# Scores ahead of other work on VectorE in the first two groups of a graph-attention kernel

## The chip, the cores and the metric

The kernel runs on one core of one Trainium2 chip. A core has five engines that run side by side, each with its own queue of instructions, and they wait for one another through semaphores. TensorE multiplies matrices into PSUM, an accumulator memory of eight banks. VectorE and ScalarE can read PSUM. [...] SyncE issues the transfers between the chip's large memory (HBM) and SBUF, the working memory. The metric is the device time of one execution in microseconds, as the median of several runs. In the profile the engines are called PE, DVE, ACT, POOL and SP, and PEld is TensorE's loading of weights, which overlaps its products.

## The reference: what is computed

There are 128 graphs of 128 nodes with 768 features each. One layer of masked attention with 12 heads of 64 features is added to the input:

```python
h = jnp.maximum(_layernorm(x, axis=-1), 0.0)
q = _split_heads(h @ Wq + bq)
k = _split_heads(h @ Wk + bk)
v = _split_heads(h @ Wv + bv)
scores = jnp.einsum('bhqd,bhkd->bhqk', q, k) / sqrt(64)
adj_e = adj[:, None, :, :]
scores = scores + beta * adj_e
scores = jnp.where(adj_e > 0, scores, -9e15)
probs = softmax(scores, axis=-1)
out = x + (einsum('bhqk,bhkd->bhqd', probs, v), heads merged)
```

Everything is in float32. About one in eight entries of adj is positive.

## The kernel before

The kernel works on groups of four graphs, 32 groups in all. A group passes through three slices: `qk0` (q and k of heads 0 to 5), `v`, and `qk1` (q and k of heads 6 to 11). In a slice the large product of activations and weights is made from 15 block products with fewer multiplications than the 18 of the plain scheme, at the cost of sums of activation blocks (`S...`) and of weight blocks (`T...`). The weight sums are made once, in the first group; the activation sums in every group. The first slice of group 0 is computed plainly with 18 products, because its sums are not there yet.

The sums of weights and of activations, all on VectorE, one instruction of 512 elements per partition each:

```python
SUMS_B = (
    ("T9", "-B01", "B12", -1), ("T2", "B01", "B02", 1), ("T2", "T2", "B22", 1), ("T10", "B10", "B12", 1),
    ("T0", "B00", "B02", 1), ("T12", "-B00", "B12", -1), ("T6", "T0", "B22", 1), ("T7", "T10", "B21", -1),
    ("T1", "T6", "B20", 1), ("T1", "T1", "B21", -1), ("T4", "T10", "B20", -1), ("T11", "B11", "B12", 1),
    ("T11", "T11", "B21", -1), ("T13", "B11", "B01", -1), ("T13", "T13", "T10", -1),
)
SC_AT = 1              # scores are issued behind product 1 of a slice
AV_AT = (5, 8, 11)     # attention blocks behind products 5, 8 and 11
HT_AT = {"A01": 0, "A00": 1, "A11": 2, "A02": 3, "A10": 4, "A12": 9}
```

(The three comments are added here; in the kernel these lines stand without them.)

A block product keeps adding into the bank of its chain (`a` to `d`). After each product the partial sum is read: the first reading of a target goes to ScalarE for q and k, every later one is an addition on VectorE. So a product waits until the reading of the earlier one of its chain is done:

```python
def product(G, sl, n, order):
    an, bn, chain, uses = PRODUCTS[n]
    ...
    nc.tensor.matmul(p[q:q + HD, i, :], lhs[:, q:q + HD], rhs, start=(first and i == 0 and c == 0), ...)     # L331
    ...
    for (r, j), sign in uses:
        ...
        elif key not in qk:
            ...
            nc.scalar.activation(t[:, i, :], p[:, i, :], AF.Identity, bias=bqk[:, i, oc:oc + 1], scale=float(sign))   # L352
        else:
            t = qk[key]
            added[G] = nc.vector.tensor_tensor(t, t, p, ALU.add if sign > 0 else ALU.subtract)    # L356
    if n == mine[-1]:
        give(banks.pop(chain))
```

The list of products gives the chain of each. For the steps that the text below speaks of: P2, P7, P11 and P14 share chain b, P0, P3, P6, P9 and P12 share chain c.

The scores of six heads take six of the eight banks at once. VectorE takes each bank out, caps the scores and adds the bias; ScalarE makes the exponential:

```python
def scores(G, u):
    order = (3 * u, 3 * u + 2, 3 * u + 1)
    ps = {(oc, i): take() for oc in order for i in range(2)}
    for oc in order:
        ...     # score matmuls, L377
        for i in range(2):
            e = es[G, oc, i] = work.tile(...)
            nc.vector.scalar_tensor_tensor(e, ps[oc, i]..., SCORE_CAP * ISCALE, biasT[G], op0=ALU.min, op1=ALU.add)   # L381
            give(ps[oc, i])
            nc.scalar.activation(e, e, AF.Exp, scale=1.0 / ISCALE)                                                    # L384
```

The bias is made from adj on VectorE, with its square on ScalarE; the maximum of the square only feeds a guard at the end (`seen_b`), which decides whether a general version has to run again:

```python
def bias_1(G, raw):
    ...
    nc.vector.transpose(a, raw...)                        # L298
    nc.vector.tensor_scalar(kp, a, 0.0, None, op0=ALU.is_gt)
    nc.vector.tensor_scalar(a, a, beta_c, ...)
    nc.gpsimd.memset(t, MASKED)
    nc.vector.copy_predicated(t, kp, a)
    nc.scalar.activation(a, a, AF.Square)                 # L305
    return a

def bias_2(G, a):
    nc.vector.tensor_reduce(bm, a, AX.X, ALU.max)         # L310
    nc.vector.tensor_tensor(seen_b, seen_b, bm, ALU.max)  # L311
```

The attention block multiplies the exponentials with V (which carries a column of ones, so that the sum comes along), and `weigh` divides:

```python
def weigh(G, oc, r, pa, o):
    nc.vector.tensor_scalar(sm, pa[:, :, HD:VE], TINY, None, op0=ALU.max)
    nc.vector.reciprocal(rs, sm)
    nc.vector.tensor_mul(o, pa[:, :, 0:HD], rs.to_broadcast([P, 4, HD]))      # L392
    for i, t in enumerate((sm, rs)):
        nc.vector.tensor_tensor(s, s, ..., ALU.max)

def attend(G, oc):
    for r in range(2):
        ...                               # matmuls, L406
        weigh(G, oc, r, pa, o[:, r])
        give(bank)
    nc.gpsimd.tensor_add(t, t, o...)      # L411
    nc.sync.dma_start(out[...], t)
```

The order of work is written as lists of what is to be issued behind which product (`then(n, f)`). The framework may move an instruction ahead on its engine when its inputs are early; `tc.issue_after(i)` holds it behind instruction `i`. In the first two groups:

```python
if G + 1 < NG:
    for g in range(GRP):
        then(6, lambda g=g: load_x(G + 1, g, (nc.sync,)))
        if G:
            then(11 + g, lambda g=g: stats(G + 1, g))                          # slice qk0
...
if G == 1:
    for n in range(8, len(SUMS_B)):
        then(n - 8, lambda n=n: sum_weights("qk0", n))                         # slice qk0
...
then(10, lambda: bias_2(0, behind_adds(bias_1, 0, adj_0)))                     # slice v of group 0
...
def transposes(n):
    with tc.issue_after(added[G].ins):
        to_hT(G + 1, int(n[1]), int(n[2]))                                     # slice qk1
if not G:
    for n in range(8):
        then(n, lambda n=n: behind_adds(sum_weights, "qk0", n))                # slice qk1
    then(13, lambda: bias_2(1, behind_adds(bias_1, 1, load_adj(1))))
```

Of the kernel before, what the change touches and what calls it, by code (L numbers as in the profile page):

```python
# [13 lines left out]
AF = mybir.ActivationFunctionType  # L14
ALU = mybir.AluOpType
AX = mybir.AxisListType

P = 128
HEADS = 12
GRP = 4  # L20
# [4 lines left out]
SCORE_CAP = 60.0  # L25
# [6 lines left out]
def kernel(  # L32
# [56 lines left out]
# [6 lines that stand above are left out]
# [6 lines left out]
SC_AT = 1  # L101
# [10 lines left out]
def direct(ctx, tc, x, adj, wq, bq, wk, bk, wv, bv, beta, out, bad):  # L112
# [10 lines left out]
    nc = tc.nc  # L123
    B, N, D = x.shape
    HD = D // HEADS
# [6 lines left out]
    ISCALE = math.sqrt(HD)  # L132
# [13 lines left out]
    xg, A, biasT, vt, qk = {}, {}, {}, {}, {}  # L146
# [51 lines left out]
    def sum_weights(sl, n):  # L198
        name, a, b, sign = SUMS_B[n]
        if (sl, name) not in wt:  # L200
            raw = [r for r, home in HOME.items() if home == name]
            wt[sl, name] = wt[sl, raw[0]] if raw else const.tile([P, 2, H2], F32, name=f"{sl}_{name}")
        if a[0] == "-":
            nc.vector.scalar_tensor_tensor(wt[sl, name], wt[sl, a[1:]], -1.0, wt[sl, b], op0=ALU.mult,
                                           op1=ALU.add if sign > 0 else ALU.subtract)
        else:
            nc.vector.tensor_tensor(wt[sl, name], wt[sl, a], wt[sl, b], ALU.add if sign > 0 else ALU.subtract)
# [80 lines left out]
    def load_adj(G):  # L288

        t = work.tile([P, GRP, NB, SQ], F32, tag="adj", name=f"adj_{G}", bufs=1)  # L290
        src = adj[G * GRP:(G + 1) * GRP].rearrange("g (b i) (a j) -> a i (g b) j", i=SQ, a=NB)
        for a in range(NB):
            nc.sync.dma_start(t[a * SQ:(a + 1) * SQ].rearrange("p g b j -> p (g b) j"), src[a])
        return t
# [13 lines left out]
    def bias_2(G, a):  # L308
        bm = stat.tile([P, GRP], F32, tag="bm", name=f"bm_{G}", bufs=1)
        nc.vector.tensor_reduce(bm, a, AX.X, ALU.max)  # L310
        nc.vector.tensor_tensor(seen_b, seen_b, bm, ALU.max)  # L311

    banks, added = {}, {}
# [43 lines left out]
        if n == mine[-1]:  # L357
            give(banks.pop(chain))

    es, xo = {}, {}  # L360

    def load_xo(G, oc):
        t = xo[G, oc] = work.tile([P, GRP, P], F32, tag="xo", name=f"xo_{G}_{oc}", bufs=3)
# [2 lines left out]
# [6 lines that stand above are left out]
                t = qk[G, f"qk{u}", g // 2, oc % 3]  # L372
                at = slice((g % 2) * N, (g % 2 + 1) * N)
                for i in range(2):
                    r = slice(i * HD, (i + 1) * HD)
                    for k in range(0, N, HD):
                        nc.tensor.matmul(ps[oc, i][k:k + HD, g * N:(g + 1) * N], t[r, 1, at][:, k:k + HD], t[r, 0, at],  # L377
                                         start=True, stop=True)
            for i in range(2):
                e = es[G, oc, i] = work.tile([P, GRP, N], F32, tag="e", name=f"e_{G}_{oc}_{i}", bufs=6)  # L380
                nc.vector.scalar_tensor_tensor(e, ps[oc, i].rearrange("p (g n) -> p g n", g=GRP), SCORE_CAP * ISCALE,  # L381
                                               biasT[G], op0=ALU.min, op1=ALU.add)
                give(ps[oc, i])
                nc.scalar.activation(e, e, AF.Exp, scale=1.0 / ISCALE)  # L384

    def weigh(G, oc, r, pa, o):

        sm = stat.tile([P, 4, 1], F32, tag="sm", name=f"sm_{G}_{oc}_{r}")
        nc.vector.tensor_scalar(sm, pa[:, :, HD:VE], TINY, None, op0=ALU.max)
        rs = stat.tile([P, 4, 1], F32, tag="rs", name=f"rs_{G}_{oc}_{r}")  # L390
        nc.vector.reciprocal(rs, sm)
        nc.vector.tensor_mul(o, pa[:, :, 0:HD], rs.to_broadcast([P, 4, HD]))  # L392
        for i, t in enumerate((sm, rs)):
            s = seen[:, i, 4 * r:4 * r + 4]
            nc.vector.tensor_tensor(s, s, t.rearrange("p b e -> p (b e)"), ALU.max)
# [95 lines left out]
    adj_0 = load_adj(0)  # L491
# [22 lines left out]
    def after(f, *args):  # L514

        with tc.issue_after(first["dve"].ins), tc.issue_after(first["pool"].ins):
            return f(*args)
# [11 lines left out]
    def behind_adds(f, *args):  # L529

        with tc.issue_after(added[0].ins):
            return f(*args)

    for G in range(NG):
        todo = attention(G - 1, 1) if G else {}

        def then(n, f):
            todo.setdefault(n, []).append(f)

        if G:  # L540
            todo.setdefault(SC_AT, []).insert(0, lambda: scores(G - 1, 1))

        if G + 1 < NG:
            for g in range(GRP):
                then(6, lambda g=g: load_x(G + 1, g, (nc.sync,)))
                if G:
                    then(11 + g, lambda g=g: stats(G + 1, g))
        if not G:
            load_weights("qk1")
            with tc.issue_after(first["dve"].ins):  # L550
                half(1, 0)
            then(1, lambda: half(1, 1))
            then(2, lambda: half(1, 2))
            for n in range(len(SUMS_A)):
                then(n + 5, lambda n=n: after(sum_acts, 0, n))
            for n in range(len(SUMS_B)):
                then(n // 2 + 5, lambda n=n: after(sum_weights, "v", n))
            plain_slice(0, "qk0", todo)
        else:
            if G == 1:  # L560
                for n in range(8, len(SUMS_B)):
                    then(n - 8, lambda n=n: sum_weights("qk0", n))
            slice_of(G, "qk0", todo)
        todo = {SC_AT: [lambda: scores(G, 0)]} if G else {}
        if G + 1 < NG:
            got = []
            at = 3 if G else 6
            for g in range(GRP):
                if not G:
                    then(g, lambda g=g: stats(G + 1, g))  # L570
                then(at + 5 + g, lambda g=g: norm(G + 1, g))
            then(at, lambda: got.extend(moments_1(G + 1, 0, GRP * NB)))
            then(at + (3 if G else 2), lambda: moments_2(G + 1, 0, GRP * NB, *got[:2]))
            if G:
                then(8, lambda: got.append(bias_1(G + 1, load_adj(G + 1))))
                then(12, lambda: bias_2(G + 1, got[2]))
            else:
                for n in range(len(SUMS_B)):
                    then(n, lambda n=n: behind_adds(sum_weights, "qk1", n))
                then(10, lambda: bias_2(0, behind_adds(bias_1, 0, adj_0)))  # L580
        slice_of(G, "v", todo)
        todo = attention(G, 0)
        if not G:
            todo.setdefault(SC_AT, []).insert(0, lambda: scores(0, 0))

        def transposes(n):
            with tc.issue_after(added[G].ins):
                to_hT(G + 1, int(n[1]), int(n[2]))

        if not G:  # L590
            for n in range(8):
                then(n, lambda n=n: behind_adds(sum_weights, "qk0", n))
            then(13, lambda: bias_2(1, behind_adds(bias_1, 1, load_adj(1))))
        if G + 1 < NG:
            for n, at in HT_AT.items():
                then(at, lambda n=n: transposes(n))
            for n, at in enumerate(SUMS_AT):
                then(at, lambda n=n: sum_acts(G + 1, n))
        if G + 1 < NG:
            slice_of(G, "qk1", todo)  # L600
            continue

        todo = {}
        for at, f, *args in (
            (0, load_xo, 0), (0, load_xo, 1), (0, load_xo, 2), (0, attend, 0), (2, attend, 2), (4, attend, 1),
            (9, scores_half, 5, 0), (10, scores_half, 4, 0), (11, attend_half, 5, 0), (12, scores_half, 3, 0),
            (12, attend_half, 4, 0), (13, scores_half, 3, 1), (13, attend_half, 3, 0), (14, scores_half, 5, 1),
            (14, attend_half, 3, 1), (14, scores_half, 4, 1), (14, attend_half, 5, 1), (14, attend_half, 4, 1),
        ):
            then(at, lambda f=f, args=args: f(G, *args))  # L610
        slice_of(G, "qk1", todo, LAST)
# [142 lines left out]
```

## Time and profile before

| | |
|---|---|
| median of 3 runs | 2917.83 us (2917.03 to 2917.94) |
| span of the profiled execution | 2913.8 us |
| TensorE's granted clock over the span | 0.998 of full speed |
| slice qk0 of group 0 (plain) | 15.96 to 48.08 us |
| slice v of group 0 | 48.08 to 74.57 us |
| slice qk1 of group 0, with scores 0 | from 74.57 us; score matmuls at 78.55 us |
| scores 1, in slice qk0 of group 1 | score matmuls at 114.94 us |
| VectorE busy, 78.5 to 84.4 us | 5.90 of 5.90 us |
| VectorE busy, 84.4 to 114.9 us | 30.50 of 30.50 us |
| VectorE busy, 158 to 190 us | 17.79 of 32.00 us |

A row of a timeline is a run of equal instructions: its start, its length, the engine, the line of the kernel, the operation, what is written and what is read, their shapes and the count. A bracket gives the idle time of the engine just before it and who ended it. A row of the table by windows gives for each engine the busy time and, in brackets, the number of instructions, in the order PE, PEld, DVE, ACT, POOL; then the granted clock of TensorE, the busy share of the DMA engines and the rate in GB/s.

### The profile page before, as it was taken

Reading aid. Unit: us, or ns where it says so; the run is one execution under the profiler, and the core shown is the slowest. Engines: PE = TensorE matmul, PEld = TensorE weight load, DVE = VectorE, ACT = ScalarE, POOL = GpSimd, SP = SyncE. Lnnn points to the kernel's source line nnn. Section 1 sums busy time; section 2 is a strip of 40 time slices with the busy share of each in tenths; the row PEclk is TensorE's granted clock in tenths of the full one; section 3 lists DMA queues with packets and bytes.
Section 4 is the critical chain, followed back from the end, with each engine's and each line's share of the span. In section 5 each row is a group of like instructions: output and inputs, shape, how many; then the busy total and the mean of one; then the engine's idle time right before and its main releaser. Section 6 shows DMA issues by size and latency. Waiting matters only on the chain.

```text
span 2913.8 us, 81848 instructions
## 1 busy us (share of the span) xinstructions
PE 2881.5 (99%) x35526; PEld 2017.0 (69%) x35526; DVE 1993.8 (68%) x5155; ACT 796.6 (27%) x1703; POOL 376.0 (13%) x307
## 2 busy tenths in 40 slices
PE   8899999999999999999999999999999999999998
PEld 6666676666676666766667666677667776666766
DVE  7866676766677666776667676677766677666765
ACT  2322222323223232222222232322323222222221
POOL 1111111111111111111111111111111111111110
PEclk9999999999999999999999999999999999999999
DMA  6211122111222212222112212122121222111211
GB/s 164 71 52 46 51 70 69 50 55 48 61 70 56 58 38 61 71 59 56 45 52 70 67 50 55 45 65 70 52 61 38 61 70 59 56 45 49 67 41 38
DMA packets 358622, 172.22 MB, mean 59 GB/s; under 512 B 84464, under 2 KB 358128, under 8 KB 358256
## 3 DMA queue, kind: packets, MB, share of 16 engines
q1 hardware_dynamic: 355392, 166.14, 21.0%
q8 instruction: 280, 4.59, 0.7%
q10 hardware_dynamic: 2864, 0.79, 0.1%
q14 instruction: 86, 0.70, 0.1%
HBM read 116.53 MB, written 50.33 MB: 57 GB/s over the span
## 4 chain that ended last, share of the span: by engine, by line
PE 81%; issue 8%; DVE 5%; DMA 2%; POOL 2%; SPq 1%; ACT 0%; ACTq 0%; POOLq 0%; DVEq 0%
PE bank L331 70%; PE bank L406 5%; PE bank L377 5%; DMA x<-in_x_dram 2%; DVE S L285 1%; PE bank L477 1%; POOL xo L411 1%; POOL rstd L261 1%; DVE qk L356 1%; DVE st L227 1%; DVE A L279 1%; DVE o L392 0%; SPq L152 0%; DVE e L381 0%; ACT x L272 0%
## 5 line engine op out<-in xcount | busy, mean ns | idle before, releaser
L331 PE MATMUL bank<-S,qk_T 128*64 128x256 f32 x7056 | 825.5, 380 | 13.3 <-DVE e L381 11.9
L331 PEld LDWEIGHTS bank<-S,qk_T 128*64 128x64 f32 x7056 | 503.9, 137 | 273.4 <-DVE e L381 16.4
L356 DVE TENSOR_TENSOR qk<-qk,bank 128x512 f32<-128x512 f32 x630 | 430.4, 683 | 347.0 <-PE bank L331 346.7
L352 ACT ACTIVATE qk<-bank,bqk 128x256 f32<-128x256 f32 x756 | 313.4, 471 | 1010.4 <-PE bank L331 870.1
L331 PE MATMUL bank<-S,qk_B 128*64 128x256 f32 x4032 | 478.1, 379 | 0.9 <-DVE qk L356 0.9
L331 PE MATMUL bank<-A,qk_T 128*64 128x256 f32 x4032 | 478.5, 379 | 0.3 <-DVE qk L356 0.3
L411 POOL TENSOR_TENSOR xo<-xo,o 128x512 f32<-128x512 f32 x189 | 256.1, 1355 | 1608.5 <-DVE o L392 1029.7
L331 PE MATMUL bank<-v_T,S 128*64 128x256 f32 x3584 | 422.7, 380 | 0.0
L384 ACT ACTIVATE e<-e 128x512 f32<-128x512 f32 x378 | 227.6, 630 | 684.4 <-DVE e L381 683.9
L347 DVE TENSOR_TENSOR v<-v,bank 128x512 f32<-128x512 f32 x320 | 220.1, 688 | 264.7 <-PE bank L331 264.6
L331 PEld LDWEIGHTS bank<-A,qk_T 128*64 128x64 f32 x4032 | 283.8, 137 | 137.3 <-DVE qk L356 0.4
L331 PEld LDWEIGHTS bank<-S,qk_B 128*64 128x64 f32 x4032 | 278.1, 137 | 129.3 <-DVE qk L356 1.4
L331 PEld LDWEIGHTS bank<-v_T,S 128*64 128x64 f32 x3584 | 252.2, 137 | 126.4 <-issue 5.7
L272 ACT ACTIVATE x<-x,shift,rstd 128x192 f32<-128x192 f32 x512 | 228.0, 533 | 343.6 <-POOL shift L263 343.6
L331 PE MATMUL bank<-v_B,S 128*64 128x256 f32 x2048 | 244.7, 380 | 0.0
L381 DVE SCALAR_TENSOR_TENSOR e<-bank,biasT 128x512 f32<-128x512 f32 x378 | 231.5, 681 | 13.5 <-PE bank L377 13.5
L331 PE MATMUL bank<-v_T,A 128*64 128x256 f32 x2048 | 238.3, 379 | 0.0
L342 DVE TENSOR_TENSOR v<-bv_b,bank 128x512 f32<-128x512 f32 x192 | 131.9, 687 | 145.8 <-PE bank L331 145.8
L406 PEld LDWEIGHTS bank<-v,e 128*64 128x64 f32 x6048 | 208.5, 138 | 27.4
L279 DVE STREAM_TRANSPOSE A<-x 128x256 f32<-128x256 f32 x384 | 215.6, 613 | 7.6 <-ACT x L272 7.4
L227 DVE BATCH_NORM_STATS2 st<-x 128x6 f32<-128x192 f32 x512 | 160.8, 349 | 76.1 <-DMA x<-in_x_dram 75.6
L406 PE MATMUL bank<-v,e 128*64 128x65 f32 x6048 | 208.3, 221 | 0.0
(79 smaller groups left out, 1724.7 us busy)
## 6 DMA issues: line engine op xcount, KB each, us to landing
x<-in_x_dram SPq DMA_DIRECT2D x504, 96.0 KB, 2.5
xo<-in_x_dram SPq DMA_DIRECT2D x189, 256.0 KB, 2.8
out_dram<-xo SPq DMA_DIRECT2D x189, 256.0 KB, 2.2
adj<-in_adj_dram SPq DMA_DIRECT2D x128, 64.0 KB, 2.4
qk_T<-in_L_gnn_Wq_dram SPq DMA_DIRECT2D x10, 128.0 KB, 3.4
qk_T<-in_L_gnn_Wk_dram SPq DMA_DIRECT2D x10, 128.0 KB, 3.4
v_T<-in_L_gnn_Wv_dram SPq DMA_DIRECT2D x5, 256.0 KB, 5.9
qk_B<-in_L_gnn_Wq_dram SPq DMA_DIRECT2D x8, 128.0 KB, 3.4
```

The source lines that it names most:

```text
L227: nc.vector.bn_stats(st[G][:, g * NB + b, :], xg[G, g][:, b, :])
L272: nc.scalar.activation(t, t, AF.Relu, bias=shift[G, n], scale=rstd[G, n])
L279: last = nc.vector.transpose(t[:, :, g * N:(g + 1) * N].rearrange("p c (b i) -> p c b i", i=SQ), src)
L331: nc.tensor.matmul(p[q:q + HD, i, :], lhs[:, q:q + HD], rhs, start=(first and i == 0 and c == 0), stop=(c == 1), skip_group_check=True)
L347: added[G] = nc.vector.tensor_tensor(o, o, got, ALU.add if sign > 0 else ALU.subtract)
L352: nc.scalar.activation(t[:, i, :], p[:, i, :], AF.Identity, bias=bqk[:, i, oc:oc + 1], scale=float(sign))
L356: added[G] = nc.vector.tensor_tensor(t, t, p, ALU.add if sign > 0 else ALU.subtract)
L377: nc.tensor.matmul(ps[oc, i][k:k + HD, g * N:(g + 1) * N], t[r, 1, at][:, k:k + HD], t[r, 0, at], start=True, stop=True)
L381: nc.vector.scalar_tensor_tensor(e, ps[oc, i].rearrange("p (g n) -> p g n", g=GRP), SCORE_CAP * ISCALE, biasT[G], op0=ALU.min, op1=ALU.add)
L384: nc.scalar.activation(e, e, AF.Exp, scale=1.0 / ISCALE)
L406: nc.tensor.matmul(pa[q:q + HD, 2 * g + i, :], es[G, oc, i][:, 2 * r + g, q:q + HD], vt[G, "v", r, h // 4][:, 4 * g + h % 4, :], start=Tru ...
L411: nc.gpsimd.tensor_add(t, t, o.rearrange("p a (b j) d -> p (a b) (j d)", j=2))
```

## The change

In the first two groups VectorE has additional work: sums of weights, and for group 1 its transposes and sums of activations in a hurry. The change orders this work so that VectorE takes the scores first. It has five parts:

- `taken[0]` remembers the last taking of scores; `behind_scores` holds work behind it. Weight sums of `qk0`, the transposes of group 1 and the statistics of group 2 go behind the scores of their slice.
- Nine weight sums in place of eight are made in slice qk1 of group 0, from product 2 on; the other six in slice qk0 of group 1, from product 2 on.
- The bias maximum of groups 0 and 1 is made a slice later than the bias itself, behind the scores.
- In group 0 the first V outputs are divided on ScalarE: four copies of 64 elements with a scale per half block, in place of one multiplication of 256 elements on VectorE.
- The rest stays as it was: the division from group 1 on, the transposes that group 1 and later groups make for the next one, the bias maximum from group 2 on.

What is computed stays the same.

```diff
@@ -357,7 +357,7 @@
         if n == mine[-1]:
             give(banks.pop(chain))
 
-    es, xo = {}, {}
+    es, xo, taken = {}, {}, {}
 
     def load_xo(G, oc):
         t = xo[G, oc] = work.tile([P, GRP, P], F32, tag="xo", name=f"xo_{G}_{oc}", bufs=3)
@@ -378,8 +378,8 @@
                                          start=True, stop=True)
             for i in range(2):
                 e = es[G, oc, i] = work.tile([P, GRP, N], F32, tag="e", name=f"e_{G}_{oc}_{i}", bufs=6)
-                nc.vector.scalar_tensor_tensor(e, ps[oc, i].rearrange("p (g n) -> p g n", g=GRP), SCORE_CAP * ISCALE,
-                                               biasT[G], op0=ALU.min, op1=ALU.add)
+                taken[0] = nc.vector.scalar_tensor_tensor(e, ps[oc, i].rearrange("p (g n) -> p g n", g=GRP), SCORE_CAP * ISCALE,
+                                                          biasT[G], op0=ALU.min, op1=ALU.add)
                 give(ps[oc, i])
                 nc.scalar.activation(e, e, AF.Exp, scale=1.0 / ISCALE)
 
@@ -389,7 +389,11 @@
         nc.vector.tensor_scalar(sm, pa[:, :, HD:VE], TINY, None, op0=ALU.max)
         rs = stat.tile([P, 4, 1], F32, tag="rs", name=f"rs_{G}_{oc}_{r}")
         nc.vector.reciprocal(rs, sm)
-        nc.vector.tensor_mul(o, pa[:, :, 0:HD], rs.to_broadcast([P, 4, HD]))
+        if G:
+            nc.vector.tensor_mul(o, pa[:, :, 0:HD], rs.to_broadcast([P, 4, HD]))
+        else:
+            for b in range(4):
+                nc.scalar.activation(o[:, b], pa[:, b, 0:HD], AF.Copy, scale=rs[:, b])
         for i, t in enumerate((sm, rs)):
             s = seen[:, i, 4 * r:4 * r + 4]
             nc.vector.tensor_tensor(s, s, t.rearrange("p b e -> p (b e)"), ALU.max)
@@ -531,6 +535,12 @@
         with tc.issue_after(added[0].ins):
             return f(*args)
 
+    def behind_scores(f, *args):
+
+        with tc.issue_after(taken[0].ins):
+            return f(*args)
+
+    early = []
     for G in range(NG):
         todo = attention(G - 1, 1) if G else {}
 
@@ -543,7 +553,9 @@
         if G + 1 < NG:
             for g in range(GRP):
                 then(6, lambda g=g: load_x(G + 1, g, (nc.sync,)))
-                if G:
+                if G == 1:
+                    then(11 + g, lambda g=g: behind_scores(stats, G + 1, g))
+                elif G:
                     then(11 + g, lambda g=g: stats(G + 1, g))
         if not G:
             load_weights("qk1")
@@ -558,8 +570,9 @@
             plain_slice(0, "qk0", todo)
         else:
             if G == 1:
-                for n in range(8, len(SUMS_B)):
-                    then(n - 8, lambda n=n: sum_weights("qk0", n))
+                for n in range(9, len(SUMS_B)):
+                    then(n - 7, lambda n=n: behind_scores(sum_weights, "qk0", n))
+                then(4, lambda: behind_scores(bias_2, 1, early[1]))
             slice_of(G, "qk0", todo)
         todo = {SC_AT: [lambda: scores(G, 0)]} if G else {}
         if G + 1 < NG:
@@ -577,23 +590,24 @@
             else:
                 for n in range(len(SUMS_B)):
                     then(n, lambda n=n: behind_adds(sum_weights, "qk1", n))
-                then(10, lambda: bias_2(0, behind_adds(bias_1, 0, adj_0)))
+                then(10, lambda: early.append(behind_adds(bias_1, 0, adj_0)))
         slice_of(G, "v", todo)
         todo = attention(G, 0)
         if not G:
             todo.setdefault(SC_AT, []).insert(0, lambda: scores(0, 0))
 
         def transposes(n):
-            with tc.issue_after(added[G].ins):
+            with tc.issue_after(added[G].ins if G else taken[0].ins):
                 to_hT(G + 1, int(n[1]), int(n[2]))
 
         if not G:
-            for n in range(8):
-                then(n, lambda n=n: behind_adds(sum_weights, "qk0", n))
-            then(13, lambda: bias_2(1, behind_adds(bias_1, 1, load_adj(1))))
+            for n in range(9):
+                then(n + 2, lambda n=n: behind_scores(sum_weights, "qk0", n))
+            then(5, lambda: behind_scores(bias_2, 0, early[0]))
+            then(13, lambda: early.append(behind_scores(bias_1, 1, load_adj(1))))
         if G + 1 < NG:
             for n, at in HT_AT.items():
-                then(at, lambda n=n: transposes(n))
+                then(at if G else max(at, SC_AT), lambda n=n: transposes(n))
             for n, at in enumerate(SUMS_AT):
                 then(at, lambda n=n: sum_acts(G + 1, n))
         if G + 1 < NG:
```

## The prediction

> **What bounds the kernel now.** I read the page's busy shares first, then TensorE's waits in the first 340 us, then the timelines of TensorE and VectorE over 78 to 128 us, then the granted clock there microsecond by microsecond. The shares:
>
> ```profile
> PE 2881.5 (99%) x35526; PEld 2017.0 (69%) x35526; DVE 1993.8 (68%) x5155; ACT 796.6 (27%) x1703; POOL 376.0 (13%) x307
> ```
>
> TensorE is busy for 2881.5 of 2913.8 us and its instruction order is the same in both programs. So only its gaps (32.3 us, of which about 16 us pass before its first product) and its slow stretches can be won. The waits of TensorE up to 340 us (us in total, times, longest):
>
> ```profile
> PE bank L238 <- DVE st L227: 7.7, 2, 5.8
> PE bank L331 <- DVE e L381: 6.9, 3, 3.6
> PE bank L331 <- DVE qk L356: 1.2, 2, 0.9
> ```
>
> The first belongs to the start-up, which the change leaves alone. The others are products (L331) that wait for a PSUM bank until VectorE has taken scores out of it (L381), or until it has added a finished partial sum to q and k (L356). Where they lie, in TensorE's timeline (start, length, in brackets the idle time before):
>
> ```profile
> 78.55 2.85 PE L377 MATMUL bank<-qk 64*64 64x128 f32 x96
> 84.48 3.67 PE L331 MATMUL bank<-S,qk_T 128*64 128x256 f32 x32 [3.08 <-DVE e L381]
> ...
> 105.04 1.95 PE L331 MATMUL bank<-A,qk_T 128*64 128x256 f32 x16 [0.27 <-DVE qk L356]
> 107.89 1.95 PE L331 MATMUL bank<-S,qk_B 128*64 128x256 f32 x16 [0.90 <-DVE qk L356]
> ...
> 121.39 6.46 PE L331 MATMUL bank<-S,qk_T 128*64 128x256 f32 x32 [3.59 <-DVE e L381]
> ```
>
> The score matmuls end at 81.40 us and TensorE stands until 84.48. After the second score block it stands for 3.59 us, and then 32 matmuls take 6.28 us (121.39 to the next row's start, 127.67) where 32 take 3.46 elsewhere. The granted clock (the column after POOL) says why:
>
> ```profile
> 119.00:120.00 1.00, 0.00 (x0) 0.00 (x0) 1.00 (x6) 0.11 (x1) 0.00 (x0) 1.00 0.15 19
> 120.00:121.00 1.00, 0.00 (x0) 0.00 (x0) 1.00 (x4) 0.00 (x0) 0.00 (x0) 0.62 0.06 8
> 121.00:122.00 1.00, 0.61 (x4) 0.43 (x6) 1.00 (x3) 0.57 (x1) 0.00 (x0) 0.50 0.00 0
> 126.00:127.00 1.00, 1.00 (x8) 0.48 (x6) 1.00 (x3) 0.34 (x1) 0.20 (x1) 0.50 0.00 0
> 127.00:128.00 1.00, 1.00 (x12) 0.70 (x10) 0.96 (x3) 0.05 (x1) 0.00 (x0) 0.97 0.14 24
> ```
>
> During the idle stretch the clock falls to half and stays there until about 127 us. VectorE's timeline shows what it did instead of taking the first scores:
>
> ```profile
> 78.03 0.69 DVE L310 TENSOR_REDUCE bm<-adjT 128x4 f32<-128x512 f32 x1 [3.48 <-ACT adjT L305]
> 79.31 0.68 DVE L347 TENSOR_TENSOR v<-v,bank 128x512 f32<-128x512 f32 x1
> 81.11 1.12 DVE L279 STREAM_TRANSPOSE A<-x 128x256 f32<-128x256 f32 x2
> 82.72 1.13 DVE L279 STREAM_TRANSPOSE A<-x 128x256 f32<-128x256 f32 x2
> 83.77 3.65 DVE L381 SCALAR_TENSOR_TENSOR e<-bank,biasT 128x512 f32<-128x512 f32 x6
> ```
>
> It stood 3.48 us in front of the bias maximum, whose square ScalarE delivers late, and only then worked off a sum of activations into V, weight sums and four transposes. From 78 to 126 us it has no idle gap.
>
> **What the Trainium skill says.** "TensorE: Matmul & The Clock Gate", section "What's actually happening", gives a free-running window of about 3.4 us: an idle window puts the clock at half, a busy one restores it. The trace agrees: 3.08 us idle kept full clock, 3.59 us lost it. "PSUM — Partial Sum Buffer", section "Engine vs sequencer instructions", says that the queues of ScalarE and VectorE are strict FIFO; the 3.48 us wait that held everything behind it is that. "ScalarE: Activation LUTs", section "What ACT_TABLE_LOAD costs", gives 186 ns + 0.833 ns per element, 93 ns more for each pointer operand, 93 ns of overlap back to back. Its 532 ns for the norms (192 elements, two pointers) fit the 533 ns in the trace. "SBUF — State Buffer", section "Who interferes with whom", says that a VectorE instruction with two SBUF inputs contends with a GpSimd one that reads SBUF. The trace has it: while GpSimd adds xo at 97.22, two sums of VectorE take 2.36 us in place of about 1.3.
>
> **The change part by part.** I number a slice's products P0 to P14; one takes 1.727 us (TensorE's row to row), an attention block 0.93.
>
> *Scores first, bias maximum out of the way.* With the maximum gone from this place, VectorE has finished its V sums and two weight sums by about 77.5 us. The first scores can be taken 1.14 us after the score matmuls begin (that lag is seen in group 1: matmuls at 153.02, taken at 154.16), so at 79.7. Six takings at 0.60 us end at 83.3. TensorE needs the first freed bank at 81.40 and has it at 80.4. The wait of 3.08 us goes: TensorE is ahead by 3.08.
>
> *Work put behind.* It must now be done between the two score blocks. Unhindered, TensorE would reach P14 at 81.40 + 12 x 1.727 + 3 x 0.93 = 104.9. P14 continues P11's bank, so it needs VectorE's addition of P11. In the new order there stand up to and with it: 6 takings, 7 additions, 9 weight sums and 9 activation sums, together 31 x 0.60 = 18.6; 12 transposes x 0.54 = 6.5; the bias maximum 0.6; four halves of attention statistics without their multiplication x 0.28 = 1.1. That is 26.8 us, from 79.7 to 106.5. GpSimd's additions of xo cross this span twice, at 1.1 us each if they meet two-input sums: 106.5 to 108.7, mean 107.6. P14 thus starts at 107.6 and not at 109.67. TensorE is 2.1 us ahead, and its waits for L356 grow from 1.2 to about 2.7.
>
> *The division on ScalarE.* The multiplication of 0.34 us leaves VectorE six times before the second scores (2.0 us; it is counted above by its absence) and six times after. ScalarE gets 48 copies of 64 elements with one pointer: by the skill's formula 186 + 93 + 53 - 93 = 239 ns each, an estimate, 11.5 us in all on an engine that is busy for 27%. The statistics of the first block come at 79.7 + 13.3 = 93.0, so eight copies end at 95.1; behind them in the queue is P6's copy to SBUF (0.84), which ends at 95.9. P9 would want that bank at 95.35: a wait of 0.5 us, which the wait at P14 swallows.
>
> *The second score block.* After P14 come two products of group 1, then scores: 107.6 + 3 x 1.727 + 0.1 = 112.9, ending at 115.75. VectorE has after P11's addition 0.6 of statistics, 2.0 of bias work, three additions and two sums (3.0): free at 113.2. The first scores are there at 112.9 + 1.14 = 114.0. It now meets neither 2.0 us of multiplications nor the statistics of group 2 (16 x 0.27 = 4.3 us, which the old order threads between the takings). So TensorE goes on at 115.75 without a wait, where it went on at 121.39: 5.6 us. No idle window, no half clock: another 6.28 - 3.46 = 2.8 us. Sum 8.4; without the contention 9.5. I take the middle, 9.0.
>
> *Afterwards.* Six weight sums and the statistics follow the takings (from 117.6). T4, needed at P8, is the second of them, and P8 starts at about 127. From 140 us on VectorE waits for TensorE in most rows, so the lead stays. The other waits for scores (5.2 us in nine places after 140 us) are in code that stays as it is.
>
> **The rivals.** *VectorE's backlog only moves the wait.* If its work between the score blocks takes 3 us more than counted, the second takings start late again, 1 to 3 us of idle return, and with over 3.4 us the half clock too. Then 3 to 5 us are left: 2913 to 2915. For it: VectorE has no gap there. Against it: 3.48 us of idling and 2.0 us of multiplications leave it, and 4.3 us of statistics move behind.
> *ScalarE becomes the step that is waited for.* If a copy costs 332 ns with no overlap, eight take 2.65 us, P9 waits 1.2 us, and later P6 of group 1 likewise: 1 to 2 us lost, 2910 to 2911. Against it: ScalarE's long gaps (18.12 us before 113.33).
> *A deferred weight sum or transpose comes late,* and TensorE waits for a product's operand: then 2910 or more. The margins are about 9 us for T4 and over 10 us for the first activation sums.
>
> **Range and chances.** 2917.83 - 9.0 = 2908.8. All waits in reach are 3.08 + 1.17 + 3.59 + 2.8 = 10.6 us, which puts the floor at 2907.2; with half a microsecond of scatter, 2906.7. The upper end takes half of the first rival: 2912.3. Two per cent are 58 us, more than all gaps of TensorE, and nothing here could cost as much: within 2% with 0.99.
>
> **What would show it.** Right: no wait of some 3 us at either score block; a granted clock of 1.00 from 78 to 130; the waits for L356 at 2 to 3 us; the first taking near 79.7 and the second block's near 114; ScalarE's copies at about 240 ns. Wrong: a wait named L381 over 1 us before 130 us, a clock below 1.00 there, or a new wait for L352, L207 or L285.

## The result and the profile after

| | before | after |
|---|---|---|
| median of 6 runs | 2916.97 us (2912.03 to 2917.94) | 2907.56 us (2905.17 to 2909.06) |
| ratio of the times, 95% interval | | 0.9970 (0.9957 to 0.9983) |
| span of the profiled execution | 2913.8 us | 2905.1 us |

The changed kernel is faster by 9.4 us, or 0.3%. That is clear of the scatter and far below 2%. The prediction was 2908.8 us.

TensorE's waits in the first 340 us of the changed kernel (us in total, times, longest). Because the change adds lines, L396 is now the division on ScalarE and L415 GpSimd's addition of xo:

```profile
PE bank L238 <- DVE st L227: 7.0, 2, 5.8
PE bank L481 <- DVE A L279: 2.2, 1, 2.2
PE bank L331 <- DVE qk L356: 1.8, 3, 0.9
PE bank L254 <- DVE dev L245: 0.5, 1, 0.5
PE bank L331 <- DVE e L381: 0.4, 1, 0.4
PE bank L331 <- ACT qk L352: 0.2, 1, 0.2
```

The waits for scores (L381) fell from 6.9 to 0.4 us. Those for additions to q and k (L356) grew from 1.2 to 1.8, and one for ScalarE is new. The timeline of TensorE shows where:

```profile
79.57 2.85 PE L377 MATMUL bank<-qk 64*64 64x128 f32 x96
82.35 3.67 PE L331 MATMUL bank<-S,qk_T 128*64 128x256 f32 x32
...
96.69 1.95 PE L331 MATMUL bank<-S,qk_B 128*64 128x256 f32 x16 [0.16 <-ACT qk L352]
...
103.38 1.95 PE L331 MATMUL bank<-A,qk_T 128*64 128x256 f32 x16 [0.36 <-DVE qk L356]
106.26 1.95 PE L331 MATMUL bank<-S,qk_B 128*64 128x256 f32 x16 [0.94 <-DVE qk L356]
108.67 3.67 PE L331 MATMUL bank<-S,qk_T 128*64 128x256 f32 x32 [0.46 <-DVE qk L356]
...
114.00 2.85 PE L377 MATMUL bank<-qk 64*64 64x128 f32 x96
116.78 3.67 PE L331 MATMUL bank<-S,qk_T 128*64 128x256 f32 x32
```

Both score blocks are followed by the next product at once: 82.35 is 2.78 us after 79.57, and 116.78 is 2.78 us after 114.00. In this execution everything stands 1.02 us later from the start on (first score matmul at 79.57 in place of 78.55; in the profiles of this study it lies between 78.34 and 80.29, whatever the kernel). The clock has a part in that too: the first 16 matmuls of the plain slice took 5.41 us here, with half clock from 15.86 to 19.27 us, and 3.72 us at full clock in the profile before. Times below are therefore counted from the first score matmul. VectorE, as far as the first score block:

```profile
76.83 0.68 DVE L207 TENSOR_TENSOR qk_T<-qk_T,qk_T 128x512 f32<-128x512 f32 x1
80.78 3.68 DVE L381 SCALAR_TENSOR_TENSOR e<-bank,biasT 128x512 f32<-128x512 f32 x6 [3.27 <-PE bank L377]
84.38 2.20 DVE L279 STREAM_TRANSPOSE A<-x 128x256 f32<-128x256 f32 x4
```

It is ready at 77.5 and stands for 3.27 us, now for the scores themselves. The granted clock (the column after POOL), where it had been half before:

```profile
120.00:121.00 1.00, 1.00 (x14) 0.64 (x10) 1.00 (x3) 0.50 (x2) 0.00 (x0) 1.00 0.00 0
121.00:122.00 1.00, 1.00 (x12) 0.65 (x10) 1.00 (x2) 0.34 (x1) 0.00 (x0) 1.00 0.00 0
126.00:127.00 1.00, 1.00 (x12) 0.69 (x10) 1.00 (x8) 0.58 (x3) 0.00 (x0) 1.00 0.00 0
```

### The profile page after: what moved, and what is told of

Same layout as the page of the kernel before. It is cut to its first block, busy times and chain, and to the rows that moved or that the text cites. A ratio compares the mean times of both kernels' runs of the same rounds, so it can differ in the third digit from the quotient of the medians.

```text
span 2905.1 us, 81884 instructions
## 1 busy us (share of the span) xinstructions
PE 2880.0 (99%) x35526; PEld 2016.3 (69%) x35526; DVE 1987.7 (68%) x5143; ACT 806.8 (28%) x1751; POOL 376.0 (13%) x307
## 4 chain that ended last, share of the span: by engine, by line
PE 81%; issue 9%; DVE 5%; DMA 2%; POOL 2%; SPq 1%; ACT 0%; POOLq 0%; DVEq 0%
PE bank L331 70%; PE bank L377 5%; PE bank L410 5%; DMA x<-in_x_dram 2%; PE bank L481 1%; POOL rstd L261 1%; POOL xo L415 1%; DVE S L285 1%; DVE qk L356 1%; DVE st L227 1%; DVE A L279 1%; DVE o L393 0%; SPq L152 0%; DVE e L381 0%; SPq L416 0%
## 5 line engine op out<-in xcount | busy, mean ns | idle before, releaser
L356 DVE TENSOR_TENSOR qk<-qk,bank 128x512 f32<-128x512 f32 x630 | 429.8, 682 | 344.9 <-PE bank L331 344.6
L352 ACT ACTIVATE qk<-bank,bqk 128x256 f32<-128x256 f32 x756 | 313.4, 471 | 992.8 <-PE bank L331 833.8
L415 POOL TENSOR_TENSOR xo<-xo,o 128x512 f32<-128x512 f32 x189 | 256.1, 1355 | 1606.9 <-DVE o L393 993.2
L381 DVE SCALAR_TENSOR_TENSOR e<-bank,biasT 128x512 f32<-128x512 f32 x378 | 231.2, 680 | 16.7 <-PE bank L377 16.7
L279 DVE STREAM_TRANSPOSE A<-x 128x256 f32<-128x256 f32 x384 | 215.5, 612 | 7.6 <-ACT x L272 7.4
```

The costliest lines, as they stand in the source:

```text
L279: last = nc.vector.transpose(t[:, :, g * N:(g + 1) * N].rearrange("p c (b i) -> p c b i", i=SQ), src)
L381: taken[0] = nc.vector.scalar_tensor_tensor(e, ps[oc, i].rearrange("p (g n) -> p g n", g=GRP), SCORE_CAP * ISCALE, biasT[G], op0=ALU.min, ...
L415: nc.gpsimd.tensor_add(t, t, o.rearrange("p a (b j) d -> p (a b) (j d)", j=2))
```

## The experiments

The best yardstick for a few microseconds is the trace, since TensorE's order is the same in all these kernels: the time from the first score matmul (s0) to the product behind it, to the second score block (s1), to the product behind that, and to the first attention matmul after it. All values are differences of starts in TensorE's timeline, in us:

| kernel | product after s0 | s1 | product after s1 | attention | median time, us |
|---|---|---|---|---|---|
| before, first profile | 5.93 | 36.39 | 42.84 | 52.58 | 2916.97 |
| before_1 | 5.93 | 37.64 | 43.81 | 50.77 | 2914.21, one run |
| before_2 | 5.92 | 37.72 | 43.87 | 53.58 | 2915.69, one run |
| after | 2.78 | 34.43 | 37.21 | 44.17 | 2907.56 |
| after_again | 2.78 | 34.41 | 37.19 | 44.15 | 2906.26 |
| bm_only | 2.78 | 33.14 | 39.33 | 46.29 | 2909.46 |
| order_only | 2.78 | 34.93 | 37.72 | 44.67 | 2907.06 |
| group1_unheld | 2.78 | 34.41 | 41.02 | 49.66 | 2911.63 |
| vector_division | 2.78 | 35.70 | 38.48 | 45.44 | 2907.71 |
| stats_only | 5.95 | 36.49 | 41.42 | 50.03 | 2912.23 |
| fill5 | 2.78 | 33.14 | 35.92 | 42.88 | 2904.62 |

Beside after_again, bm_only, order_only and group1_unheld the kernel before had a median of 2913.40 us in 42 runs (2909.62 to 2916.71); beside vector_division, fill5 and stats_only 2913.51 us in 33 runs (2911.08 to 2916.84).

**The changed kernel once more, without an edit (after_again).**

> The changed kernel itself, as the yardstick for the runs beside it. All theories: about 9 us below the kernel before; score block of group 1 followed by products without a wait; granted clock 1.00 from 78 to 130 us.

Ratio 0.9973 (0.9962 to 0.9984): 7.1 us between the medians. No wait followed the score blocks, and the clock was 1.00 from 78 to 130 us.

**The bias maximum alone (bm_only).**

```diff
+                then(4, lambda: behind_scores(bias_2, 1, early[1]))
...
-                then(10, lambda: bias_2(0, behind_adds(bias_1, 0, adj_0)))
+                then(10, lambda: early.append(behind_adds(bias_1, 0, adj_0)))
...
-            then(13, lambda: bias_2(1, behind_adds(bias_1, 1, load_adj(1))))
+            then(5, lambda: behind_scores(bias_2, 0, early[0]))
+            then(13, lambda: early.append(behind_adds(bias_1, 1, load_adj(1))))
```

`then(4, ...)` stands in slice qk0 of group 1, `then(5, ...)` in slice qk1 of group 0.

> The kernel before, with nothing changed but the bias maximum of groups 0 and 1, made a slice later. Theory of the prediction (the backlog of VectorE decides): the first wait of 3.1 us is gone, since VectorE no longer stands still for 3.5 us; but the 16 statistics and the multiplications still stand before or between the second takings, TensorE arrives there earlier and so waits longer, 4 to 5 us, and again at half clock for some 6 us (2.8 us lost). Sum: only about 3 us below the kernel before. Rival theory (the bias maximum was the whole of it): about 9 us below, as the full change.

The first wait is gone, and the second stays, as TensorE's timeline shows:

```profile
111.48 2.85 PE L377 MATMUL bank<-qk 64*64 64x128 f32 x96
117.67 3.67 PE L331 MATMUL bank<-S,qk_T 128*64 128x256 f32 x32 [3.34 <-DVE e L381]
```

The wait is 3.34 us, less than the 4 to 5 expected, and in this execution it was not followed by half clock (32 matmuls span the usual 3.67). The ratio to the kernel before is 0.9985 (0.9978 to 0.9992): 3.9 us between the medians, of the 7.1 us that the full change brings in the same set of runs. The rival falls: the bias maximum is not the whole of it.

**Everything but the bias maximum (order_only).** Against the changed kernel:

```diff
-                then(4, lambda: behind_scores(bias_2, 1, early[1]))
...
-                then(10, lambda: early.append(behind_adds(bias_1, 0, adj_0)))
+                then(10, lambda: bias_2(0, behind_adds(bias_1, 0, adj_0)))
...
-            then(5, lambda: behind_scores(bias_2, 0, early[0]))
-            then(13, lambda: early.append(behind_scores(bias_1, 1, load_adj(1))))
+            then(13, lambda: bias_2(1, behind_scores(bias_1, 1, load_adj(1))))
```

> The changed kernel with the bias maximum back at its old place in groups 0 and 1, so that VectorE stands still again until ScalarE's square is there. Theory of the prediction: VectorE in the changed kernel stands still for 3.3 us at that place anyway (it waits for the first scores), so waiting there for the square costs nothing but some tenths: 0 to 0.5 us above the changed kernel, first scores taken at about 80.6 us counted from the same start as before. Rival (the bias maximum was what held VectorE up): about 3 us above the changed kernel.

VectorE stands 3.47 us for the square, as before, and takes the first scores 1.95 us behind their first matmul (80.09):

```profile
79.56 0.69 DVE L310 TENSOR_REDUCE bm<-adjT 128x4 f32<-128x512 f32 x1 [3.47 <-ACT adjT L305]
...
82.04 3.67 DVE L381 SCALAR_TENSOR_TENSOR e<-bank,biasT 128x512 f32<-128x512 f32 x6
```

That is still early enough: the product behind the first scores comes at 2.78. Against after_again this kernel is 0.5 us slower (s1 at 34.93 against 34.41, attention at 44.67 against 44.15), and P9 waits 0.96 us for ScalarE's reading (L352). So either part alone removes the first wait; the move of the bias maximum adds 0.5 us to the new order.

**Group 1 without its holds (group1_unheld).**

```diff
-                if G == 1:
-                    then(11 + g, lambda g=g: behind_scores(stats, G + 1, g))
-                elif G:
+                if G:
                     then(11 + g, lambda g=g: stats(G + 1, g))
...
-                    then(n - 7, lambda n=n: behind_scores(sum_weights, "qk0", n))
+                    then(n - 7, lambda n=n: sum_weights("qk0", n))
```

> The changed kernel, but in group 1 the last six weight sums and the statistics of group 2 are not held behind the scores. Theory: three weight sums and 11 of 16 statistics move ahead of the second takings (4.8 us of VectorE); TensorE waits about 3.9 us after the second score block and then runs at half clock for about 6 us, 2.8 us lost: 6 to 7 us above the changed kernel. Rival without the clock's part: 3.9 us above, clock 1.00 throughout. Rival in which VectorE has room there: less than 1 us.

VectorE's timeline shows the statistics in front of the second takings and between them:

```profile
117.10 2.95 DVE L227 BATCH_NORM_STATS2 st<-x 128x6 f32<-128x192 f32 x11
119.95 1.28 DVE L381 SCALAR_TENSOR_TENSOR e<-bank,biasT 128x512 f32<-128x512 f32 x2
121.14 0.88 DVE L227 BATCH_NORM_STATS2 st<-x 128x6 f32<-128x192 f32 x3
```

TensorE waits 3.76 us, then the clock is half for 3.4 us and not 6. To the attention block it costs 49.66 - 44.15 = 5.5 us, of which the clock 49.66 - 41.02 - 6.96 = 1.7. The medians say 5.4, of the 7.1 us of the full change: without the holds in group 1 only 1.8 of it are left. The shares of different runs overlap (bm_only alone had 3.9) and can't be added. Which of the two holds does more, that of the weight sums or that of the statistics, was not tried in the changed kernel.

**The division back on VectorE (vector_division).**

```diff
-        if G:
-            nc.vector.tensor_mul(o, pa[:, :, 0:HD], rs.to_broadcast([P, 4, HD]))
-        else:
-            for b in range(4):
-                nc.scalar.activation(o[:, b], pa[:, b, 0:HD], AF.Copy, scale=rs[:, b])
+        nc.vector.tensor_mul(o, pa[:, :, 0:HD], rs.to_broadcast([P, 4, HD]))
```

> The changed kernel with the division of group 0 back on VectorE. Theory: 0.34 us six times; four of them stand before the addition of P11, which TensorE waits for, so P14 is 1.4 us later, and the rest is hidden behind the scores: 1.4 us above the changed kernel, waits for L356 up from 1.8 to about 3.2 us. Rival (the division is off the path): equal to the changed kernel.

By the trace 45.44 - 44.15 = 1.3 us more, with waits for L356 of 3.4 us; by the medians, which are from two different sets of runs, 1.45. The rival falls: the division was on the path, because P12 to P14 wait for VectorE (2.65, 0.30 and 0.46 us).

**The statistics alone (stats_only).** Against the kernel before:

```diff
-                if G:
+                if G == 1:
+                    then(11 + g, lambda g=g: behind_scores(stats, G + 1, g))
+                elif G:
                     then(11 + g, lambda g=g: stats(G + 1, g))
```

> The kernel before with one thing changed: the statistics of group 2 are held behind the scores in group 1. Theory: nine statistics (2.4 us) leave the way of the second takings, TensorE waits about 1 us there in place of 3.6 and keeps its full clock: 2.6 + 2.8 = 5.4 us below the kernel before, more than half of the full change. Rival without a clock effect: 2.6 us below.

A miss: 0.9995 (0.9987 to 1.0004), no gain that can be told from none. VectorE stands again where it had not before, in front of the bias maximum of group 1:

```profile
118.06 0.74 DVE L304 COPY_PREDICATED biasT<-kp,adjT 128x512 f32<-128x512 uint8 x1
119.56 0.69 DVE L310 TENSOR_REDUCE bm<-adjT 128x4 f32<-128x512 f32 x1 [0.76 <-ACT adjT L305]
120.36 3.67 DVE L381 SCALAR_TENSOR_TENSOR e<-bank,biasT 128x512 f32<-128x512 f32 x6
```

TensorE's second wait fell to 2.09 us and not to 1, and half clock follows this wait as it follows the first one of 3.09 us, each for 3.4 us; behind the second score block that costs 50.03 - 41.42 - 6.96 = 1.65 us. A limit of 3.4 us of idle time cannot be right.

**Five weight sums ahead of the first scores (fill5).**

```diff
-            for n in range(9):
+            for n in range(5):
+                then(0, lambda n=n: behind_adds(sum_weights, "qk0", n))
+            for n in range(5, 9):
                 then(n + 2, lambda n=n: behind_scores(sum_weights, "qk0", n))
```

> The changed kernel with five of the nine weight sums that it holds behind the first scores put ahead of them, into the 3.3 us in which VectorE waits for the first scores. Theory (P14 waits because VectorE's work between the two score blocks is too long by 1.8 us): that work is 3.0 us shorter, the first taking is not later, the waits for L356 fall from 1.8 us to 0.3 or less, the second takings keep their lead: 1.5 to 2 us below the changed kernel. Rival (the sums ahead of the scores delay the first taking): a wait at the first score block of 1 us or more and no gain.

VectorE's pause in front of the first taking shrinks from 3.27 to 0.25 us, and the taking comes no later (1.21 us behind the score matmuls in both):

```profile
80.87 3.68 DVE L381 SCALAR_TENSOR_TENSOR e<-bank,biasT 128x512 f32<-128x512 f32 x6 [0.25 <-PE bank L377]
```

L356 is waited for only 0.5 us. The gain is 44.15 - 42.88 = 1.3 us by the trace, a little under the expected 1.5. The median, 2904.62 us (ratio 0.9971, 0.9960 to 0.9982), is the lowest of all, but by time alone the two versions, timed in different sets of runs, can't be told apart.

**Two sweeps of the wait (idle_sweep, idle_sweep2), and the kernel before twice more without an edit (before_1, before_2).** In the sweeps the first taking of a later group's scores is repeated to the same tile. The second sweep holds each taking behind the last:

```diff
+                for n in range(again + 1):
+                    ...
+                        taken[0] = nc.vector.scalar_tensor_tensor(e, ps[oc, i]..., SCORE_CAP * ISCALE, biasT[G], op0=ALU.min, op1=ALU.add)
```

> The changed kernel; in groups 3 to 26 the first taking of the first score block is repeated 4, 6, 7, 8, 9, 10, 12, 14 times in turn before it counts (the same result is written again), so that TensorE waits there for about 0.6 us per repeat less 1.0: 1.4, 2.6, 3.2, 3.8, 4.4, 5.0, 6.2, 7.4 us, three groups of each. Theory of a fixed limit: full clock after waits below 3.4 us, and after every wait above it half clock for some 6 us, 2.8 us more. Rival of a free-running window of 3.4 us that must be idle as a whole: waits of 3.4 to 6.8 us are followed by half clock only in part of the cases, more often the longer they are, those above 6.8 us always.

> As the sweep before, but the repeats and the takings behind them are held in a row, so that no other bank comes free earlier: in groups 3 to 26 the first taking of the first score block is made 5, 7, 8, 9, 10, 11, 13, 15 times in turn, and TensorE waits about 1.4, 2.6, 3.2, 3.8, 4.4, 5.0, 6.2, 7.4 us, three groups of each. Theory formed from the runs so far (half clock followed waits of 2.1, 3.1, 3.6 and 3.8 us and not others of 3.1 and 3.3 us): the clock is set anew at the ends of fixed windows of 3.4 us, which do not follow the kernel, and falls when more than about 55% of a window was idle. Then all cold stretches begin at times that differ by whole multiples of 3.41 us and last whole multiples; waits of 1.4 us never cool, waits of 2.6 to 3.2 us in a part of the cases, waits over 5.2 us always. Rival, a fixed limit of 3.4 us of idle time: 2.6 and 3.2 never, 3.8 and more always, beginning 3.4 us after TensorE stopped.

Both failed in what they were made for: TensorE had other products to run in the gap, and no wait got longer than 1.63 us in the first and 1.94 in the second. The first has no half clock between start-up and end, the second still has five stretches of it. Their starts and lengths, from the granted clock:

```
start      length     distance from the first, in units of 3.4133 us
331.19     3.41       0
1071.88    3.41       217.0
1167.45    3.41       245.0
1815.98    3.41       435.0
1911.56    3.41       463.0
```

> The kernel before once more, for another position against the windows. Window theory: the two waits of 3.1 and 3.6 us are there again in the same length, but the half clock may follow none, one or both of them, for 3.4 or 6.8 us; the time goes with it, 1.7 us for each window. Fixed limit: exactly as in the first profile, half clock after the second alone.

> The kernel before a third time. Both theories as for the second: under the window theory the cold stretches may differ from both other profiles, under the fixed limit they are the same in all three.

TensorE's timeline of before_1 at its two waits:

```profile
85.82 6.54 PE L331 MATMUL bank<-S,qk_T 128*64 128x256 f32 x32 [3.08 <-DVE e L381]
...
123.70 3.67 PE L331 MATMUL bank<-S,qk_T 128*64 128x256 f32 x32 [3.32 <-DVE e L381]
```

and of before_2:

```profile
85.73 6.62 PE L331 MATMUL bank<-S,qk_T 128*64 128x256 f32 x32 [3.08 <-DVE e L381]
...
123.68 6.42 PE L331 MATMUL bank<-S,qk_T 128*64 128x256 f32 x32 [3.31 <-DVE e L381]
```

The waits are nearly the same in all three profiles of this kernel. Half clock follows the second alone, the first alone, or both, each time for 6.83 us. The fixed limit falls.

## Why the prediction was right, step by step

*First scores.* Taken 1.21 us after the score matmuls begin (1.14 predicted), no wait. Right.

*Work between the score blocks.* P14 and the product behind it are the row at 108.67; less the later start of 1.02 that is 107.65, where 107.6 was predicted. The count behind it was right: from the first taking at 80.78 to the end of P11's addition at 108.62, VectorE's timeline has the 31 takings, additions and sums and the 12 transposes that were counted, and they take 27.8 us, 1.0 more than the 26.8 without contention. The waits for L356, "to about 2.7", read as 1.8 in the list. By the starts P14 is 2.7 us late: from 95.43, 101.92, 103.38 and 106.26 to the next product, TensorE needs 0.33, 0.53, 1.15 and 0.68 us more than the 0.93 of an attention block or the 1.73 of a product. But the first of these is P9, which waits for ScalarE; VectorE's part is 2.4 us, and it lies at P12, P13 and P14, not at P14 alone. The list counts from modelled ends of matmuls and misses part of such gaps.

*GpSimd.* It does cross this span twice, at about half the size I took:

```profile
98.07 1.17 DVE L285 TENSOR_TENSOR S<-S,A 128x512 f32<-128x512 f32 x1
...
103.82 1.19 DVE L207 TENSOR_TENSOR qk_T<-qk_T,qk_T 128x512 f32<-128x512 f32 x1
...
110.90 1.50 DVE L301 TENSOR_SCALAR adjT<-adjT,beta_c 128x512 f32<-128x512 f32 x1
```

GpSimd's additions in the same time:

```profile
95.98 2.71 POOL L415 TENSOR_TENSOR xo<-xo,o 128x512 f32<-128x512 f32 x1 [23.76 <-ACT o L396]
103.18 1.28 POOL L415 TENSOR_TENSOR xo<-xo,o 128x512 f32<-128x512 f32 x1 [4.49 <-ACT o L396]
110.84 1.27 POOL L415 TENSOR_TENSOR xo<-xo,o 128x512 f32<-128x512 f32 x1 [6.38 <-ACT o L396]
```

Two instructions of VectorE of usually 0.68 us took 0.5 more each; the mean of 0 and 2.2 that I took, 1.1, was about the sum. That was luck: neither of the two cases that I averaged occurred. In the first meeting GpSimd's own addition took 2.71 us in place of 1.28. A third meeting, which I had left out, cost 1.0 us at L301 (0.47 in the profile before). It moved the second takings to 1.45 us behind their score matmuls, and stayed hidden because TensorE was busy with scores for 2.78 us.

*ScalarE.* Eight copies take 1.75 us, 219 ns each, where 239 was the estimate from the formula of the Trainium skill ("ScalarE: Activation LUTs", section "What ACT_TABLE_LOAD costs"). One wait of 0.16 us in the list, 0.33 by the starts, for 0.5 predicted.

*Second scores.* The product behind them comes 37.21 us after s0; before 42.84, so 5.63 us where 5.6 was predicted. To the attention block 8.41 us, which is the predicted sum with contention, 8.4.

*The clock.* Here the step was right for one profile only. I read "3.08 us idle kept full clock, 3.59 us lost it" as a limit near 3.4 us and counted the 2.8 us as a fixed part of the kernel before. The wait after the first block cools in two of three profiles as well. There it costs little: before_1 reaches s1 only 1.25 us later than the first profile, its second wait is shorter (3.32 for 3.59), and its products after s1 stand 0.97 us later, because a slower TensorE then waits less for VectorE (no wait for L356 between the score blocks, in place of 1.2 us). After the second block the 2.8 us are lost in full (9.74 and 9.71 from product to attention in place of 6.96). So the trace gain to the attention block is 8.4, 6.6 or 9.4 us, depending on which profile of before is taken. That the medians differ by 9.4 us in one set of runs and 7.1 in another fits this. So does the granted clock over the whole span, which is known for each of the 42 runs of before beside after_again: the 3 runs with 0.999 took 2911.5 us on average, 25 with 0.998 took 2912.9, 11 with 0.997 took 2914.6, and 3 with 0.996 took 2915.3. Start-up and end add to this spread, and only three executions of before have been seen in a trace. That 9.4 us were measured so near to the 9.0 is therefore partly luck: beside 42 runs of before the same change brought 7.1.

*Afterwards.* The lead stays. From the attention block to the start of the last product TensorE takes 2767.6 to 2770.7 us in all these kernels, 2768.3 to 2770.7 in the three profiles of before and 2769.1 and 2769.3 in the two of the changed kernel. Within this spread the gain lies wholly in the first 130 us.

*Rivals.* The backlog that only moves the wait is what bm_only and group1_unheld show. In the full change it did not happen because of the holds in group 1: without them TensorE waits 3.76 us at the second score block. With the maximum or the division put back alone (order_only, vector_division) the product behind the second scores still comes 2.79 and 2.78 us after them. ScalarE as the step that is waited for cost 0.33 us at P9 and not 1 to 2, and no deferred sum or transpose came late: no wait of TensorE between 78 and 140 us names L207, L285 or L279.

## What to carry to other kernels

When one engine works through a backlog while another waits for it at two places, removing the first wait brings the second one nearer: count the work between the two places, not the wait. An engine in strict order should take first what another engine waits for, and its pauses are room for the work that was pushed back (fill5). And a wait of 2 to 4 us on TensorE cost up to 2.8 us more than its length here, by chance. The scatter of the times is in keeping with that, 2904.10 to 2909.06 us in 14 runs of the changed kernel and 2909.62 to 2917.94 in 48 before, but with so unequal numbers of runs it isn't shown to be narrower.

## What was unexpected of the hardware

The Trainium skill's page "TensorE: Matmul & The Clock Gate", section "What's actually happening", speaks of an idle window of about 3.4 us. The runs agree with a free-running window of 3.413 us: starts of half clock in one execution lie 10 (stats_only), 11 (before_2), 217, 245, 435 and 463 windows (idle_sweep2) apart, and between start-up and end it lasts one or two windows. They differ in how idle the window must be. Idle time inside the window that ended where the half clock began, from the start of the wait, its end and the window's edge: 1.93 to 1.94 us (idle_sweep2, five times), 2.03 (group1_unheld), 2.05 and 2.11 (stats_only), 2.07 and 2.25 (before_2), 2.09 (before_1), 2.44 (before). Windows with 1.28, 1.66, 1.80 and 1.99 us idle kept full clock.

With each execution's own window edges, the same can be counted for all 13 traces from 22 us to the last product. Of 10,958 windows at full clock, 12 were followed by half clock, those just named. Of the others, one had 1.99 us idle (before_1), and none of the rest more than 1.81. Idle time counts from modelled ends of matmuls, so the border lies near 1.9 to 2.0 us in these kernels, less than 60% of the window. It is not a rule for idle time alone: at the very end, among the small matmuls of the last attention block, half clock began after windows with 1.39 (fill5), 1.82 (stats_only) and 1.86 us idle (idle_sweep). Why is not shown. Half clock ended with the next window if TensorE worked through nearly all of it (at most 0.04 us idle), and lasted a second window where the wait reached 0.8 to 1.2 us into the first.
